# Layer norms, filters, feed and inverse transforms placed beside other stages, the spectral layer run by output parity, and pools that wait per tile

## The chip, the cores and the metric

The kernel runs on one core of a Trainium2 chip. Times are microseconds (us) of device time for one execution; the kernel before has a median of 3496.31 us over three runs. A profile is one execution taken by the hardware profiler. The engines are called PE (matmul; PEld is its weight load), DVE (vector), ACT (scalar, with the exponential), POOL and SP (which here only issues DMAs).

## The reference, cut to what matters

Two batches of 4096 tokens with 128 channels, all in float32:

```python
# layer 0: group norm, then 4 heads of 32 channels with 2-D rotary positions
xi  = group_norm(x)                               # (b, c, 4096)
q, k, v = split(w_qkv @ xi + b_qkv)               # q, k rotated and scaled
w   = softmax((q.T @ k).astype(float16))
x   = xi + w_proj @ (w @ v) + b_proj
# layer 1
t = x.transpose()                                 # (b, 4096, 128)
n = layer_norm(t)
t = t + softmax(n @ n.T) @ n                      # one head of 128, no weights
u = layer_norm(t)
t = t + sum_i weight[i] * pad(stu(u[:, :4096 // 2**i], i))   # weight: hard one-hot over 4
# stu: 16 filters phi_k convolved causally with u (and with u times (-1)^t),
#      mixed by two sets of 16 matrices, plus three taps M_u on u, u[t-1], u[t-2]
out = t.transpose()
```

The weights are a straight-through one-hot, so that the four branches become one with mixed matrices and a mask.

## The kernel before

The tokens of a batch are kept as `tok[b]`, 32 blocks of 128 tokens (partition = token). One program runs these stages one after another, on a matmul engine that executes in program order.

**Layer 0** (L146-346). Four units (batch, pair of heads). Each unit has 2 heads x 4 chunks of 1024 queries; for each of 32 key blocks two score matmuls (L315), one exp over 128x1024 (L323) and two weighted sums into `acc` (L282). Preparing the next unit (`rotate`, `values`) is a generator that is advanced by one step in every third key block (L335): `beside`. The last unit has none beside it. `rotate` loads a table `tab` (512 KB) through SP's queue (L181). `project` brings a finished chunk back to tokens (L261-265), eight matmuls `po`.

**Layer 1, attention** (L576-768). After layer 0 come the filter transforms (`ph`, L604-614: eight records of PE, copies on DVE, one store to DRAM as `tables`), the branch weights and coefficients, then `normalise` for both batches (L712): statistics by block, `pow` on POOL (L84), 32 normed blocks (L627), 32 transposes `yT` (L719) with copies on ACT. `self_attend` (L723) takes eight chunks of 512 queries; per pair of key blocks four f32 matmuls `y` (L742), two exps of 512 (L747) and, one pair later, four weighted sums `oacc` (L735). At each chunk's end come two of the sixteen `matrices` steps, which load `raw` through ACT's queue (L702) and sum it on DVE into `mx`. Then the residual, 32 operations on DVE (L766).

**Layer 1, feed** (L770-831). Per batch: layer norm into `un`, transforms of 512 columns `pf` (L781) stored to DRAM as `rows`, transposes of `un` and `tok` (L800, L801), three taps `ar` (L819) and the sum into `out[b]`. In program order feed 0 comes between the two attentions and feed 1 between attention 1 and the spectral layer.

**Spectral layer** (L841-958). Per batch eight chunks `ch` of 4 frequencies in each quarter. A chunk loads `tt` from `tables` and `ut` from `rows`, then runs four steps (output parity `ro`, stream `s`). A step is `convolve` (for each of 4 w: four matmuls of 32 rows into two 2-bank tiles `cv`, copied into `x` by DVE and ACT, L889) and `mix` (16 f32 matmuls of 512 columns, L899, accumulating both s in `acc`), which runs one step late, four matmuls after each w. After the second s `acc` is copied to `oh[ro]` (L905). After a batch's last step `back` (L910) transposes `oh` (`vt`), copies to `v`, applies the inverse transform `bk` (L929), adds to `out[b]` and stores it. In the PSUM pool `cv` has three tiles of two banks and `acc` two of one. The `tt` and `ut` loads go through SP, 10 for each half chunk (the page counts 256 and 384).

The order on each engine is set at build time by the program order and a planner that places an instruction when its inputs are due; each engine then runs its list in order and waits on semaphores. SP's DMAs use eight semaphores in turn, so that a DMA waits for the one eight before it. Pools that reuse memory of a closed pool wait for that whole pool.

Of the kernel before, what the change touches and what calls it, by code (L numbers as in the profile page):

```python
# [12 lines left out]
F32 = mybir.dt.float32  # L13
# [6 lines left out]
P = 128  # L20
# [9 lines left out]
NK = 16  # L30
# [28 lines left out]
def conv_attn_hybrid(ctx: ExitStack, tc: tile.TileContext, io):  # L59
# [26 lines left out]
    def group_norm(b, tok, bank, p1):  # L86


        xi = p1.tile([P, L], F32, tag="xi", name=f"xi{b}")
        xn = p1.tile([P, L], F32, tag="xn", name=f"xn{b}")  # L90
# [55 lines left out]
    def layer0(tok):  # L146
        with ExitStack() as l0:
            psum = l0.enter_context(tc.tile_pool(name="l0_psum", bufs=2, space=bass.MemoryType.PSUM))
            p1 = l0.enter_context(tc.tile_pool(name="l0_1", bufs=1))
            p2 = l0.enter_context(tc.tile_pool(name="l0_2", bufs=2))  # L150

            def bank(name):
                return psum.tile([P, 512], F32, tag="ms", name=name)
# [14 lines left out]
            def prepare(b, pr, xn):  # L168
# [9 lines left out]
                def rotate(i, hi, lo):  # L178
                    cols = bass.ts(i, 512)
                    tab = p2.tile([P, 2, 512], F32, tag="tab", name=f"tab{u}_{i}")  # L180
                    nc.sync.dma_start(tab, io["rot"][pr][:, :, cols])  # L181
# [88 lines left out]
            norm = group_norm(0, tok, bank, p1)  # L270
# [22 lines left out]
            def chain(*parts):  # L293
                for p in parts:
                    yield from p

            last = None
            for n, (b, pr) in enumerate(units):
                if n + 1 < len(units):
                    nxt = units[n + 1]  # L300
                    if nxt[1] == 0:
                        norm = group_norm(nxt[0], tok, bank, p1)
                        xn = next(norm)
                        after = prepare(*nxt, xn)
                        beside = chain(beside, norm, after[3], to_tokens(nxt[0], tok, xn, bank))
                    else:
                        after = prepare(*nxt, xn)
                        beside = chain(beside, after[3])
                for g in range(2):
# [35 lines left out]
            for _ in done:  # L345
                pass


    def layer0_any(tok):

        with ExitStack() as l0:
            p1 = l0.enter_context(tc.tile_pool(name="l0_1", bufs=1))
            p2 = l0.enter_context(tc.tile_pool(name="l0_2", bufs=2))
            p3 = l0.enter_context(tc.tile_pool(name="l0_3", bufs=3))

            psum = l0.enter_context(tc.tile_pool(name="l0_psum", bufs=2, space=bass.MemoryType.PSUM))

            def pair_bank(name):
                return psum.tile([P, 2, 512], F32, tag="st", name=name, bufs=2)

            def acc_bank(name):
                return psum.tile([P, 512], F32, tag="acc", name=name, bufs=1)

            def bank(name):
                return psum.tile([P, 512], F32, tag="ms", name=name, bufs=3)
# [14 lines left out]
            def normed(b):  # L380
                steps = group_norm(b, tok, bank, p1)
                xn = next(steps)
                for _ in steps:
                    pass
                for _ in to_tokens(b, tok, xn, bank):
                    pass
                return xn
# [168 lines left out]
            for n, (b, pr) in enumerate(units):  # L556
# [9 lines left out]
                k, v = k2, v2  # L566


    tables = dram.tile([NF, 2, 2, 2 * TROW], F32, name="tables")
    rows = [dram.tile([2, DROWS, NF, C], F32, name=f"rows{b}") for b in range(B)]  # L570

# [4 lines left out]
    def layers(st, layer0):  # L576
        held = st.enter_context(ExitStack())
        keep = held.enter_context(tc.tile_pool(name="keep", bufs=1, side="right"))

        tok = [keep.tile([P, NI, C], F32, name=f"tok{b}") for b in range(B)]  # L580
        layer0(tok)

        psum_1 = st.enter_context(ExitStack())
        psum = psum_1.enter_context(tc.tile_pool(name="psum", bufs=2, space=bass.MemoryType.PSUM))

        def pair_bank(name):
            return psum.tile([P, 2, 512], F32, tag="st", name=name, bufs=2)

        def acc_bank(name):
            return psum.tile([P, 512], F32, tag="acc", name=name, bufs=1)  # L590

        def bank(name):
            return psum.tile([P, 512], F32, tag="ms", name=name, bufs=3)

        fw = keep.tile([P, 4, NF], F32, name="fw")
        nc.sync.dma_start(fw, io["fw"])
        with tc.tile_pool(name="tab", bufs=1) as pt_:
            phi = pt_.tile([P, 2, TROW], F32, name="phi")  # L600
            nc.sync.dma_start(phi, io["phi"])
            tb = pt_.tile([P, 2, 2, 2 * TROW], F32, name="tb")
            tbr = tb.rearrange("w s i (o c k) -> w s i c o k", c=2, k=NK)
            for s in range(2):  # L604
                for c in range(2):
# [3 lines left out]
                    nc.vector.tensor_copy(tbr[:, s, 0, c], ph)  # L609
                    if c == 0:  # L610
                        nc.vector.tensor_copy(tbr[:, s, 1, 1], ph)
                    else:
                        nc.vector.tensor_scalar(tbr[:, s, 1, 0], ph, -1.0, None, ALU.mult)
            nc.sync.dma_start(tables, tb)


        def layer_norm(pool, src, dst, u, eps=1e-5):

            st = pool.tile([P, NT, 6], F32, tag="lst", name=f"lst{u}")
            mv = pool.tile([P, NT, 2], F32, tag="lmv", name=f"lmv{u}")  # L620
            for t in range(NT):
                nc.vector.bn_stats(st[:, t, :], src[:, t, :])
                nc.vector.bn_aggr(mv[:, t, :], st[:, t, :])
            rs = pool.tile([P, NT], F32, tag="lrs", name=f"lrs{u}")
            rstd_of(rs, mv[:, :, 1], 1.0, eps, NT)
            for t in range(NT):
                nc.vector.tensor_scalar(  # L627
                    dst[:, t, :], src[:, t, :], mv[:, t, 0:1], rs[:, t : t + 1], ALU.subtract, ALU.mult
                )

        ffw = st.enter_context(tc.tile_pool(name="ffw", bufs=1))
        mx = ffw.tile([P, NK, 2, C], F32, name="mx")
        gw = ffw.tile([P, 2, P], F32, name="gw")

        out = [ffw.tile([P, L], F32, name=f"out{b}") for b in range(B)]

        with ExitStack() as l1:
            p1 = l1.enter_context(tc.tile_pool(name="l1_1", bufs=1))

            def branch_weights(once):  # L640

                lg = p1.tile([P, 2, NBR], F32, name="lg")
                nc.gpsimd.dma_start(lg[:, 0, :], io["log_weights"].partition_broadcast(P))
                nc.gpsimd.dma_start(lg[:, 1, :], io["gumbel"].partition_broadcast(P))
                z = p1.tile([P, NBR], F32, name="z")
                nc.vector.tensor_tensor(z, lg[:, 0, :], lg[:, 1, :], ALU.add)
                zm = p1.tile([P, 1], F32, name="zm")
                nc.vector.tensor_reduce(zm, z, AX.X, ALU.max, negate=True)  # L650
                zs = p1.tile([P, 1], F32, name="zs")
                soft = p1.tile([P, NBR], F32, name="soft")
                nc.scalar.activation(soft, z, AF.Exp, bias=zm, accum_out=zs)
                nc.vector.reciprocal(zs, zs)
                nc.vector.tensor_scalar(soft, soft, zs, None, ALU.mult)
                sm = p1.tile([P, 1], F32, name="sm")
                nc.vector.reduce_max(sm, soft, axis=AX.X)
                top = p1.tile([P, NBR], F32, name="top")
                nc.vector.tensor_scalar(top, soft, sm, None, ALU.is_equal)
                free = p1.tile([P, NBR], F32, name="free")  # L660
                nc.vector.memset(free, 1.0)
                for i in range(1, NBR):
                    nc.vector.scalar_tensor_tensor(
                        free[:, i : i + 1], top[:, i - 1 : i], 0.0, free[:, i - 1 : i], ALU.is_equal, ALU.mult
                    )
                nc.vector.tensor_tensor(top, top, free, ALU.mult)
                wbr = p1.tile([P, NBR], F32, name="wbr")
                nc.vector.tensor_tensor(wbr, top, soft, ALU.subtract)
                nc.vector.tensor_tensor(wbr, wbr, soft, ALU.add)
                ends = once.tile([P, NBR, P], F32, name="ends")  # L670
                nc.gpsimd.dma_start(ends, io["ends"].partition_broadcast(P))
                mask = p1.tile([P, P], F32, name="mask")
                weighted_sum(mask, ends, top)
                return wbr, mask

            def weighted_sum(dst, src, w):

                nc.vector.tensor_scalar(dst, src[:, 0], w[:, 0:1], None, ALU.mult)
                for i in range(1, NBR):
                    nc.vector.scalar_tensor_tensor(dst, src[:, i], w[:, i : i + 1], dst, ALU.mult, ALU.add)  # L680

            mu = p1.tile([P, NU, C], F32, name="mu")
# [406 lines left out]
```

## Time and profile before

| | us |
|---|---|
| median of three runs | 3496.31 (3494.68 to 3497.91) |
| the profiled execution | 3495.54 |
| its span | 3493.7 |
| PE busy in it | 3345.4 |
| ACT busy | 1668.9 |
| DVE busy | 924.1 |
| POOL busy | 36.3 |

The granted PE clock is 0.983 of full speed on average. Stages in the span, read from the timeline:

| stretch, us | stage |
|---|---|
| 0 to 50 | loads, group norm, first preparation |
| 50 to 1114 | layer 0, four units |
| 1114 to 1188 | last projection, filters, coefficients, both norms, first y |
| 1188 to 1616 | attention 0 |
| 1616 to 2111.5 | attention 1, with feed 0 at its start |
| 2111.5 to 2227 | residual 1, feed 1, first convolve |
| 2227 to 2829.5 | spectral, batch 0 |
| 2829.5 to 2860 | inverse transform of batch 0 |
| 2860 to 3455 | spectral, batch 1 |
| 3455 to 3493.7 | inverse transform of batch 1, stores |

A busy time is the time in which the engine had an instruction in flight; for PE the ends are modelled, so a busy PE is not a PE at its peak. An idle gap costs time only on the engine that the rest waits for. The groups of waits name the instruction that waited, and the instruction or DMA that ended the wait.

### The profile page before, as it was taken

The numbers are of one execution on the slowest core, as the hardware profiler recorded it, in microseconds if no ns is written. First come the engines' busy times: TensorE is split into PE (matmuls) and PEld (weight loads), VectorE is DVE, ScalarE is ACT, GpSimd is POOL, SyncE is SP. The second block draws the span as 40 slices with busy tenths as digits, with TensorE's granted clock in tenths as the row PEclk, the third lists the DMA queues.
The fourth block names the chain that finished last, engine by engine and source line by source line (L and its number), as shares of the span: only waits on it lengthen the run. The fifth ranks groups of instructions, "written<-read, shape, count | busy, mean of one in ns | idle before, by whom it ended". The sixth has DMA issues, their size and how long they took to land.

```text
span 3493.7 us, 31758 instructions
## 1 busy us (share of the span) xinstructions
PE 3345.4 (96%) x12040; PEld 1542.3 (44%) x12040; DVE 924.1 (26%) x2010; ACT 1668.9 (48%) x2407; POOL 36.3 (1%) x36
## 2 busy tenths in 40 slices
PE   6999999999998799999999996899999999999998
PEld 3555555555554344444444442333333353333334
DVE  6621721611112620003100004222222232222222
ACT  2799799899997344444344442122222212222221
POOL 0000000000000100000000000000000000000000
PEclk9999999999999899999999998899999999999999
DMA  5300300300001110001000001423322222233300
GB/s 150 97 19 1 91 7 1 85 1 1 1 1 30 55 55 0 0 0 30 20 0 0 0 0 50 67 37 50 47 34 34 34 58 34 34 43 50 41 0 26
DMA packets 113796, 112.03 MB, mean 32 GB/s; under 512 B 17809, under 2 KB 77601, under 8 KB 113506
## 3 DMA queue, kind: packets, MB, share of 16 engines
q1 hardware_dynamic: 93056, 95.60, 14.6%
q10 hardware_dynamic: 19698, 11.81, 1.1%
q0 software_dynamic: 880, 2.50, 0.3%
q8 instruction: 97, 1.59, 0.2%
q14 instruction: 65, 0.53, 0.1%
HBM read 78.19 MB, written 14.88 MB: 27 GB/s over the span
## 4 chain that ended last, share of the span: by engine, by line
PE 83%; ACT 9%; DVE 4%; DMA 2%; issue 1%; POOL 1%; SPq 0%; ACTq 0%; POOLq 0%; DVEq 0%
PE m L899 27%; PE y L742 12%; PE oacc L735 12%; ACT e L323 9%; PE s L315 9%; PE cv L885 8%; PE acc L282 8%; PE po L261 1%; PE ar L819 1%; PE bk L929 1%; PE pv L206 1%; PE pb L183 1%; PE pa L190 1%; PE pf L781 1%; DVE tok L766 0%
## 5 line engine op out<-in xcount | busy, mean ns | idle before, releaser
L323 ACT ACTIVATE e<-s 128x1024 f16<-128x1024 f32 x1024 | 976.1, 1033 | 128.6 <-PE s L315 125.7
L899 PE MATMUL m<-x,mx 128*128 128x512 f32 x2048 | 947.8, 606 | 0.0
L889 ACT COPY x<-cv 128x1024 f32<-128x1024 f32 x256 | 259.1, 1012 | 944.7 <-PE cv L885 930.7
L899 PEld LDWEIGHTS m<-x,mx 128*128 128x128 f32 x2048 | 369.0, 190 | 561.3 <-issue 549.2
L315 PE MATMUL s<-qs,ks 128*128 128x512 f16 x2048 | 607.8, 379 | 6.1 <-ACT e L323 2.6
L282 PE MATMUL acc<-e,v 128*97 128x512 f16 x2048 | 604.5, 379 | 1.4 <-ACT e L323 1.0
L747 ACT ACTIVATE ey<-y,nshift 128x512 f32<-128x512 f32 x512 | 347.3, 683 | 525.8 <-PE y L742 523.7
L889 DVE COPY x<-cv 128x1024 f32<-128x1024 f32 x256 | 313.3, 1224 | 849.0 <-PE cv L885 849.0
L742 PE MATMUL y<-yT 128*128 128x512 f32 x1024 | 483.3, 594 | 0.0
L735 PE MATMUL oacc<-ey,y 128*128 128x512 f32 x1024 | 480.3, 593 | 0.0
L282 PEld LDWEIGHTS <-v 128*97 128x97 bf16 x2048 | 253.0, 124 | 215.1 <-issue 5.1
L885 PE MATMUL cv<-tt,ut 32*128 32x512 f32 x2048 | 310.6, 649 | 16.1 <-DMA ut<-rows 14.8
L735 PEld LDWEIGHTS oacc<-ey,y 128*128 128x128 f32 x1024 | 194.4, 190 | 242.0 <-issue 234.6
L742 PEld LDWEIGHTS y<-yT 128*128 128x128 f32 x1024 | 193.2, 191 | 232.9 <-issue 232.9
L315 PEld LDWEIGHTS <-ks 128*128 128x128 f16 x2048 | 199.8, 98 | 215.8 <-issue 108.8
L885 PEld LDWEIGHTS cv<-tt,ut 32*128 32x128 f32 x2048 | 86.5, 185 | 217.8 <-issue 205.7
L263 DVE RECIPROCAL rec<-po 128x1 f32<-128x1 f32 x256 | 42.7, 167 | 504.1 <-PE po L261 502.6
L756 DVE COPY oT<-oacc 128x512 f32<-128x512 f32 x16 | 11.0, 689 | 614.7 <-PE oacc L735 614.7
L261 PEld LDWEIGHTS po<-wp,accs 97*128 97x128 f32 x512 | 92.0, 192 | 37.9 <-DVE accs L290 9.2
L261 PE MATMUL po<-wp,accs 97*128 97x129 f32 x512 | 99.2, 282 | 4.4 <-DVE t L185 2.5
L747 ACT ACTIVATION_READ_ACCUMULATOR ey<-y,nshift 128x1 f32 x512 | 100.3, 196 | 0.0
L265 DVE SCALAR_TENSOR_TENSOR tok<-po,rec,tok 128x128 f32<-128x128 f32 x256 | 87.3, 348 | 6.8
(138 smaller groups left out, 1091.2 us busy)
## 6 DMA issues: line engine op xcount, KB each, us to landing
tt<-tables SPq DMA_DIRECT2D x256, 128.0 KB, 4.3
tab<-in_rot SPq DMA_DIRECT2D x32, 512.0 KB, 4.1
ut<-rows SPq DMA_DIRECT2D x384, 32.0 KB, 4.6
qs<-term SPq DMA_DIRECT2D x128, 64.0 KB, 2.0
ks<-term SPq DMA_DIRECT2D x128, 64.0 KB, 2.0
rows<-uh SPq DMA_DIRECT2D x64, 128.0 KB, 1.9
raw<-in_mpp ACTq DMA_DIRECT2D x16, 256.0 KB, 2.9
raw<-in_mpm ACTq DMA_DIRECT2D x16, 256.0 KB, 3.3
```

The lines of the kernel that those rows point to most:

```text
L261: nc.tensor.matmul(po, accs[:, t // 4, bass.ts(t % 4, P)], wp[:, h, :], start=True, stop=True)
L263: nc.vector.reciprocal(rec, po[:, C:])
L265: nc.vector.scalar_tensor_tensor(dst, po[:, :C], rec, dst, ALU.mult, ALU.add)
L282: nc.tensor.matmul(acc[: NV * CH + 1, q, :], v[:, t, g, :], e[:, q, :], start=(t == 0), stop=(t == NT - 1))
L315: nc.tensor.matmul(ps[:, q, :], ks[:, g, bass.ts(t, P)], qs[:, g, bass.ts(2 * c + q, 512)], start=True, stop=True,)
L323: nc.scalar.activation(e, ps, AF.Exp, scale=SCORE_SCALE)
L735: nc.tensor.matmul(acc, y[:, t, :], e[:, h, :], start=(t == 0), stop=(t == NT - 1))
L742: nc.tensor.matmul(ps[:, h, :], yT[:, bass.ts(t, P)], yT[:, bass.ts(i, 512)], start=True, stop=True)
L747: nc.scalar.activation(e[:, h, :], ps[:, h, :], AF.Exp, bias=nshift, accum_out=den[:, t, i : i + 1])
L885: nc.tensor.matmul(pu[:, h, :], ut[grp, w, q, :], tt[grp, w, s, :], start=True, stop=True)
L889: (nc.scalar.copy if g2 else nc.vector.tensor_copy)(x[:, :, at : at + 64].rearrange("d k (h c) -> d k h c", h=2), pu.rearrange("d h (c k) ...
L899: nc.tensor.matmul(acc, mx[:, k, s, :], x[:, k, :], start=(s == 0 and k == 0), stop=(s == 1 and k == NK - 1))
```

## The change

The sequence of stages stays, but much of what stood between them becomes generators that the attention and spectral loops advance by one step.

- All pools wait for the reuse of memory per tile. Layer 0 and attention share one PSUM pool (`st` 2 x 2 banks, `acc` 2 banks, `ms` 2 banks), and group norm's `xi`, `xn` share a pool with batch 0's `y` and `yT`.
- `normalise(0)` is advanced by layer 0's last unit, with DVE copying `yT`.
- Attention takes 1024 queries a chunk, one exp of 1024 columns per key block, and calls `next(beside)` in each of its 4 x 32 steps: `normalise(1)`, the filters and the matrices beside attention 0; the residual of batch 0 and feed 0 beside attention 1.
- The feed is cut in steps of four blocks. Its result is stored to DRAM (`base`) and loaded back (`had`) by `back`.
- The spectral layer runs by (batch, parity, chunk, s). `tt` and `ut` are loaded in every step, so 512 + 512 loads. `acc` and the new `bk` have one bank each. Feed 1 is advanced beside (0, 0), and `back` of each (batch, parity) beside the next one; the last has nothing beside it. At the end of each (batch, parity) the late mix and what is left beside are drained.
- The `tab` loads move from SP's queue to POOL's, the `raw` loads from ACT's to SP's.

```diff
+    def pool(stack, name, bufs=1, **kw):
+        return stack.enter_context(tc.tile_pool(name=name, bufs=bufs, reuse_waits="tile", **kw))
...
                     tab = p2.tile([P, 2, 512], F32, tag="tab", name=f"tab{u}_{i}")
-                    nc.sync.dma_start(tab, io["rot"][pr][:, :, cols])
+                    nc.gpsimd.dma_start(tab, io["rot"][pr][:, :, cols])
...
+                else:
+                    beside = beside_last()
                 for g in range(2):
...
+        def normalise(b, p, ytag, yttag):
...
+            def steps():
+                stats = layer_stats(p, tok[b], f"a{b}")
+                mv = next(stats)
+                yield from stats
+                for i in range(NQ):
+                    for t in range(4 * i, 4 * i + 4):
+                        normed(y[:, t, :], tok[b][:, t, :], mv, t)
+                    yield
+                    pt = bank(f"yT{b}_{i}")
+                    for t in range(4):
+                        nc.tensor.transpose(pt[:, bass.ts(t, P)], y[:, 4 * i + t, :], ident)
+                    nc.vector.tensor_copy(yT[:, bass.ts(i, 512)], pt)
+                    yield
...
+            late = None
+            for c in range(L // 1024):
+                acc = psum.tile([P, 2, 512], F32, tag="acc", name=f"oacc{b}_{c}", bufs=1)
+                for t in range(NT):
+                    ps = psum.tile([P, 2, 512], F32, tag="st", name=f"y{b}_{c}_{t}")
...
+                    nc.scalar.activation(e, ps, AF.Exp, bias=nshift, accum_out=den[:, t, c : c + 1])
+                    if late is not None:
+                        weigh(*late)
+                        if t == 0:
+                            close(c - 1, acc0)
+                    late = (acc, t, e)
+                    next(beside, None)
+                acc0 = acc
...
+        def feed(b, p, bank):
+            stats = layer_stats(p, tok[b], f"f{b}")
...
+            def taps(i, uT):
...
+                nc.scalar.copy(oc, pt)
+                yield
+                pa = bank(f"ar{b}_{i}").rearrange("p (t c) -> p t c", c=C)
+                for n in range(NU):
+                    nc.tensor.matmul(pa, mu[:, n, :], uT[:, 2 - n : 6 - n, :], start=(n == 0), stop=(n == NU - 1))
+                    if n + 1 < NU:
+                        yield
+                nc.vector.tensor_tensor(oc, pa, oc, ALU.add)
+                nc.sync.dma_start(base[b][:, 4 * i : 4 * i + 4, :], oc)
+                yield
...
+                o, den = attend(0, p1, *ys[0], chain(steps, filters(p), matrices(p)))
...
+                o, den = attend(1, p1, *ys[1], chain(residual(0, p1, o, den), feed(0, p, bank)))
+            for _ in residual(1, p1, o, den):
+                pass
...
+            tt = pi.tile([P, WC, 2 * BP * NK], F32, tag="tt", name=f"tt{u}", bufs=3)
+            ut = pi.tile([P, WC, C], F32, tag="ut", name=f"ut{u}", bufs=4)
...
+        def back(b, ro, oh, outs, p):
...
+            for p4 in range(BP // 4):
+                nc.sync.dma_start(had, baser[:, ro, 4 * p4 : 4 * p4 + 4, :])
...
+                for c in range(2):
+                    pt = one_bank(f"vt{u}_{c}").rearrange("p (q c) -> p q c", c=C)
+                    for q in range(4):
+                        nc.tensor.transpose(pt[:, q, :], ohr[:, c, BP - 1 - 4 * p4 - q, :], ident)
+                    (nc.scalar.copy if c else nc.vector.tensor_copy)(v[:, c, :, :], pt)
+                    yield
+                pt = one_bank(f"bk{u}").rearrange("p (q j) -> p q j", j=P)
+                for q in range(4):
+                    for c in range(2):
+                        nc.tensor.matmul(pt[:, q, :], v[:, c, q, :], gw[:, c, :], start=(c == 0), stop=(c == 1))
+                nc.vector.tensor_tensor(outr[:, ro, 4 * p4 : 4 * p4 + 4, :], pt, had, ALU.add)
+                yield
...
+        beside = feed(1, late_pool, one_bank)
+        for b in range(B):
+            for ro in range(2):
+                oh = po.tile([P, L], F32, tag="oh", name=f"oh{b}_{ro}")
+                for ch in range(NCH):
+                    acc = pc.tile([P, 512], F32, tag="acc", name=f"m{b}_{ro}_{ch}")
+                    for s in range(2):
+                        tt, ut = chunk(b, ro, ch, s)
...
+                        for _ in convolve(u, tt, ut, x):
+                            next(late, None)
+                            next(beside, None)
+                        late = mix(ch, s, x, acc, oh)
+                for _ in chain(late, beside):
+                    pass
...
+                beside = back(b, ro, oh, outs, late_pool)
+        for _ in beside:
+            pass
```

## Prediction

> **What bounds the kernel now.** I read the page's slices first, then busy time by windows cut where the stages meet, then the waits of the tensor engine, then the timeline at two seams.
>
> ```profile
> PE   6999999999998799999999996899999999999998
> PEclk9999999999999899999999998899999999999999
> ```
>
> The tensor engine is the bound nearly everywhere, and it dips in four places: at the start, near slice 13, near slice 25 and at the end. The granted clock dips with it.
>
> ```profile
> 850.00:1114.00 264.00, 263.19 (x1245) 141.34 (x1243) 44.98 (x156) 260.57 (x276) 0.00 (x0) 1.00 0.00 1
> 1114.00:1188.00 74.00, 37.28 (x124) 20.57 (x125) 52.46 (x264) 15.37 (x37) 16.32 (x9) 0.72 0.18 58
> 1188.00:1616.00 428.00, 428.00 (x1019) 190.09 (x1017) 45.55 (x110) 178.61 (x494) 0.00 (x0) 1.00 0.06 19
> 1616.00:2111.50 495.50, 488.53 (x1209) 220.37 (x1207) 52.51 (x167) 202.18 (x538) 5.53 (x2) 1.00 0.03 9
> 2111.50:2227.00 115.50, 67.74 (x196) 29.90 (x196) 45.24 (x148) 21.60 (x30) 5.43 (x1) 0.76 0.40 75
> 2860.00:3455.15 595.15, 595.15 (x2005) 222.67 (x2004) 158.19 (x133) 129.51 (x131) 0.00 (x0) 1.00 0.23 34
> ```
>
> Columns: window, length, busy time of PE, PEld, DVE, ACT, POOL, granted clock, DMA share, GB/s. Steady attention and steady spectral work leave PE no gap. The two seams, 1114-1188 (layer norms and filters between layer 0 and attention 0) and 2111.5-2227 (residual and feed of batch 1 before the spectral layer), hold only 37 and 68 us of PE in 190. The last unit of layer 0 is held by ACT too: 260.57 of 264.
>
> ```profile
> PE pf L781 <- DVE un L627: 28.1, 2, 22.5
> PE yT L719 <- issue: 24.2, 1, 24.2
> PE gn_mean L103 <- DVE gmv L99: 19.5, 1, 19.5
> PE cv L885 <- DMA ut<-rows: 14.8, 3, 7.4
> ```
>
> The largest waits of PE. Three of the four lie in those seams; gn_mean is the kernel's head, which the change hardly touches.
>
> ```profile
> 3418.00 1.14 PE L885 MATMUL cv<-tt,ut 32*128 32x512 f32 x8
> 3419.07 3.70 PE L899 MATMUL m<-x,mx 128*128 128x512 f32 x8
> 3422.70 1.14 PE L885 MATMUL cv<-tt,ut 32*128 32x512 f32 x8
> 3422.81 0.69 DVE L905 COPY oh<-m 128x512 f32<-128x512 f32 x1 [2.41 <-PE m L899]
> 3423.77 3.70 PE L899 MATMUL m<-x,mx 128*128 128x512 f32 x8
> ```
>
> Start, length, engine, line: one w of the spectral layer starts every 4.70 us, so a step of four w is 18.8 us, and 64 steps are 1203.2.
>
> **The sum, by stretches.** PE's work is priced by start spacing: an f32 matmul record of 512 columns 0.4285 us (two records a matmul), a 128-column transpose 0.11. The number of matmuls does not change; what changes is what stands between them.
>
> *Layer 0's end to attention 0's end* took 1616.0-1114.0 = 502.0. In the changed program's instruction order the statistics, normed blocks and 32 transposes of batch 0 stand between layer 0's last scores, attention's first y follow the last acc, and batch 1's norm, the filters and the matrices come one step at a time between y and oacc. What is left there: 1024 records x 0.4285 = 438.8, o transposes 32 x 0.11 = 3.5, yT of batch 1 3.5, filters 8 x 0.42 = 3.3 and the last projection 2.6: 451.7, so -50.3. The cover is 128 steps of 3.43 us on PE, of which one 1024-wide exp takes ACT about 1.23 (1.03, the L323 row, plus a 0.20 read); DVE's 8.2 us of statistics and 8.3 of normed blocks are small beside them. Without the cover the 45 us of gap come back. The transposes moved into layer 0 cost 3.5 at face value: ACT and PE are both full there; between 0 (the 3.4 us in which ACT idles take them) and 8 (each of 8 groups also delays an exp by 0.5). A wait for POOL's pow (5.43 us) stands ahead of transposes two steps later, about level with it; I add 2 for such waits, range 0 to 6. Net -45.
>
> *Attention 1* took 495.5. Work: 438.8 + 3.5 + feed 0 (pf 32 and ar 48 records x 0.4285, 64 transposes, pl 0.4: 41.7) = 484.0, plus 2 for the same waits: -9.5. Feed's 75 steps fit in 128.
>
> *From 2111.5 to the end* took 1382.2. Afterwards:
> - Start. The first x copy on DVE stands behind the o copies (3 us) and 32 residual operations (0.266 each, 8.5), and the next ones between 8.2 us of statistics and a normed block that waits for the 5.43 us pow. Adding two steps' copies (8 x 1.22 = 9.8) and 1.0 for that block: DVE needs 36 us, in which PE has 14.5 to do. Loss 21.5; between 12 (residual alone in the way) and 30 (the statistics of the next blocks ahead as well).
> - 64 steps 1203.2, feed of batch 1 41.7 within the first 16 of them.
> - Three inverse transforms beside the next steps: 32 transposes and 64 records of bk (14.6 us for 128 in the tail): 3.5 + 7.3 = 10.8 each, 32.4.
> - The three ends of a (batch, parity), where the last mix is drained before the next cv. The first has the rest of feed 1 (11 of 75 steps do not fit in 64) in series with its one PSUM bank: 21.5 us to the next mix, of which 15 is work, so 6.5. The others 4 each (x copies at 1.22 a w, no mix beside). 14.5 in all, between 0 and 25.
> - Tail: only one parity is left, but over one bank in series: per block vt 0.65, copy 0.75, vt 0.65, copy 0.7, eight bk 2.0, add 1.2 = 5.95, four times and a first copy: 24.5. From the last add to the end 11.0 as now (3482.7 to 3493.7). 35.5, against 38.5 now.
>
> Sum 1348.8, -33.4.
>
> *The single accumulator.* Its two banks become one, so the first mix of a step waits for L905's copy. The rows above: copy ends at 3423.50, next mix starts at 3423.77, 0.27 to spare. Cost between 0 and 32 x 1.0 us (if DVE or ACT is in a 1.2 us copy or add when it is due); I take 3, because the copy is queued ahead of the next x copy. Behind it stand all sixteen mixes, so this stall would go straight to the end.
>
> *Loads.*
>
> ```profile
> tt<-tables SPq DMA_DIRECT2D x256, 128.0 KB, 4.3
> tab<-in_rot SPq DMA_DIRECT2D x32, 512.0 KB, 4.1
> ut<-rows SPq DMA_DIRECT2D x384, 32.0 KB, 4.6
> ```
>
> (Tile, queue, count, KB, us to landing.) tt doubles to 512 loads, ut becomes 512: 16 a step. A burst of ten takes SP 5.65 us in the timeline, so 16 take 9.0 of the step's 18.8, two steps ahead of use; the share, 0.23 to 0.29, would come near 0.5. The rows and base stores of feed 1 stand among them in SP's order and wait for ACT and DVE, but the loads beside them are for two steps later: nothing, unless a load is over 37 us late. The 32 raw loads go from ACT's queue to SP's during attention 0, a pair at a time (2.9 and 3.3 us to landing there now); mx is needed only 500 us later, so nothing. The feed's result makes a trip to DRAM (16 stores and 16 loads of 256 KB, on SP too), each a whole (batch, parity) ahead of its use: nothing. The 32 tab loads leave SP for POOL, behind the xi loads there; nothing else of weight waits on POOL. xi landed in 8.1 us from POOL and 8.7 from SP, so I take 0, between -3 and +8 (eight exposed loads, 1 us each, in the head).
>
> The Trainium skill has a rule against that move ("SBUF — State Buffer", section "SBUF: two separate sides"): loads issued by GpSimd have descriptors written in software, and a two-port VectorE operation locks it out, 620 ns becoming 3100. No row here shows it. By that rule, an estimate, the eight loads of the head would be 2.5 us late each, and the sum up to 20 higher.
>
> The windows at 0.72 and 0.76 are the clock's row. "TensorE: Matmul & The Clock Gate" (Part 1) has the array at half rate until one window of about 3.4 us was busy. By it, an estimate, each of the five idle places left would cost 1.7 more, 8.5 on the sum; I price no such term.
>
> In all -45 - 9.5 - 33.4 + 3 = -85 against the profiled execution's 3495.54 (span 3493.7), which is 0.8 under the median of 3496.31: **3411** on the median.
>
> **Rivals.**
> - *More hidden than I charge:* start 12, ends 0, layer 0's transposes and the waits free: 9.5 + 14.5 + 3.5 + 4 + 3 = 34 less, 3377. For: DVE's low share. Against: the order of DVE at the start.
> - *The spectral seams and the single bank take back a third:* 32 x 1.0 instead of 3, start 30, ends 25: +29 + 8.5 + 10.5 = 3459 at worst, about 3445. For: 0.27 us of slack is thin with other work on DVE. Against: that slack was there in every step.
> - *Slower: the spectral loads become the bound.* At most eight DMAs are under way on SP's semaphores, so a step needs 16/8 landings. It decides above 18.8 + 85/64 = 20.1 us a step, 1.26 a load, a landing of 10.1 us instead of 4.5. At 11.2 us a step is 22.4: 64 x 3.6 = +230, 3641. For: in the crowded head tab landed in 4.1 to 14.4 us, median 7.5. Against: the spectral stage moves only 41 GB/s, the head 169.
> - *It does not do what it says:* a norm or feed still stands ahead of the next stage on an engine. Both big seams kept, the smaller ends give about 3490.
>
> **How the numbers follow.** Forecast 0.62, more hidden 0.12, a third back 0.14, slower 0.09, not as said 0.03. No change means within 0.2%, 7 us: only the last case and the edge of the slower one, 0.02. Faster 0.90, slower 0.08. The range leaves out the slower case and the last, and reaches into the two near ones: 3375 to 3450.
>
> **What would show it.** PE gaps at the two big seams gone, with about 20 us at the spectral start behind DVE; y and oacc back to back at 3.43 us; steps of 18.8 with mix waiting under 0.3 for oh; cv waiting for no DMA; tail near 35. Wrong if steps are longer than 19.5, if PE waits for tt, or if layer 0 ends over 8 us later.

## The result and the profile after

The changed kernel takes 3985.61 us (3981.06 to 3993.36, four runs) against 3497.11 for the kernel before in the same session: 1.14 times as long, 95% interval 1.138 to 1.142. The forecast of 3411 and its range were wrong, and in sign.

The page's slices of the kernel after, PE's busy tenths and its granted clock:

```profile
PE   6999999999998999999999999999999999999997
PEclk9999999999999999999989998987798777877777
```

The dips of PE at the two big seams are gone. In their place the clock falls in the last third, where PE looks busy. The stretches of the kernel after, in the columns of the windows before, cut where its own stages meet:

```profile
1115.00:1582.70 467.70, 456.70 (x1103) 204.11 (x1102) 84.47 (x284) 154.68 (x258) 5.53 (x2) 0.99 0.14 32
1582.70:2067.90 485.20, 485.20 (x1205) 219.28 (x1203) 49.15 (x172) 168.86 (x282) 5.53 (x2) 1.00 0.05 16
2130.00:2430.00 300.00, 300.00 (x1001) 119.06 (x1000) 84.74 (x103) 67.87 (x78) 0.00 (x0) 1.00 0.42 73
3055.00:3260.00 205.00, 186.16 (x388) 70.86 (x388) 32.00 (x27) 24.88 (x25) 0.00 (x0) 0.75 0.27 39
3950.20:3991.50 41.30, 19.87 (x97) 16.75 (x96) 6.83 (x8) 2.93 (x5) 0.00 (x0) 0.70 0.18 65
```

Both attentions are done at 2067.9 instead of 2111.0: 43 us were won up to there. The first parity of the spectral layer (third row) gives PE 3.3 records a microsecond at full clock; a later stretch (fourth row) 1.9 at 0.75. From the last `oacc` to the end the kernel before took 1383 us, the changed one 1924. All of the loss is there.

The length of a step is easiest to read off the copies of `oh`, one for every two steps (a pair). One in the kernel before, whose next is the row at 3422.81 that the prediction shows, then two neighbours in the kernel after:

```profile
3385.19 0.58 ACT L905 COPY oh<-m 128x512 f32<-128x512 f32 x1 [2.56 <-PE m L899]
```

```profile
3085.03 0.69 DVE L937 COPY oh<-m 128x512 f32<-128x512 f32 x1 [4.92 <-PE m L931]
3152.56 0.59 ACT L937 COPY oh<-m 128x512 f32<-128x512 f32 x1 [20.64 <-PE m L931]
```

Times between such copies in us, within a (batch, parity):

| stretch | before | after |
|---|---|---|
| (0,0), feed 1 beside | 37.6 | 42.8 |
| (0,1), first four pairs after its first | 37.6 | 43.6, 46.7, 39.3, 68.2 |
| later | 37.6 | 56.7 to 68.2, mostly near 68 |

A late step is 34.1 us, not 18.8. One of them in the timeline of the kernel after (start, length, engine, line, records, idle before), with weight loads and SP's rows left out:

```profile
3112.36 6.28 PE L931 MATMUL m<-x,mx 128*128 128x512 f32 x14
3118.57 1.98 PE L920 MATMUL cv<-tt,ut 32*128 32x512 f32 x8
3119.76 1.23 DVE L922 COPY x<-cv 128x1024 f32<-128x1024 f32 x1 [6.01 <-PE cv L920]
3121.04 1.13 PE L920 MATMUL cv<-tt,ut 32*128 32x512 f32 x4 [0.49 <-DVE x L922]
3122.21 1.23 DVE L922 COPY x<-cv 128x1024 f32<-128x1024 f32 x1 [1.23 <-PE cv L920]
3123.49 7.38 PE L920 MATMUL cv<-tt,ut 32*128 32x512 f32 x16 [1.33 <-DVE x L922]
3125.83 1.01 ACT L922 COPY x<-cv 128x1024 f32<-128x1024 f32 x1 [27.55 <-PE cv L920]
3127.49 1.01 ACT L922 COPY x<-cv 128x1024 f32<-128x1024 f32 x1 [0.65 <-PE cv L920]
3129.20 1.01 ACT L922 COPY x<-cv 128x1024 f32<-128x1024 f32 x1 [0.69 <-PE cv L920]
3129.26 1.23 DVE L922 COPY x<-cv 128x1024 f32<-128x1024 f32 x1 [5.82 <-PE cv L920]
3130.90 1.01 ACT L922 COPY x<-cv 128x1024 f32<-128x1024 f32 x1 [0.69 <-PE cv L920]
3131.97 2.08 PE L931 MATMUL m<-x,mx 128*128 128x512 f32 x2 [1.10 <-ACT x L922]
```

Before, four m followed every w, and the copies lay under them. Here nearly all of a step's cv come in one block: PE runs up to three PSUM tiles ahead, then at the pace of the copies, DVE's first and ACT's four after, and the m that should cover them have been used up or wait for the block's last copy. From 3118.57 to 3131.97 PE does work worth about 4 us: 28 records of cv, of which eight took 1.14 us before. The two records of m behind the block take 1.0 us each instead of 0.43: the clock has been halved.

The list of PE as built, one line a step (a, b: a half of cv of the first and second group of rows; M: one m), shows the same before anything runs:

```
(0,0) chunk 3, s 1   aabbMMMMaabbMMMMaabbMMMMaabbMMMM
(0,1) chunk 2, s 0   aaMbMMMaabMMMbbMaabbMMMMaabbMMMM
(0,1) chunk 5, s 0   aMMMMMMMMaMMMMMMMbaabaabbbbaabbM
(1,1) chunk 5, s 0   aMMMMMMMMaMMMMMMMbaabaabbbbaabbM
```

The trace runs cv and m in the same order. One half of cv slips behind four m from (0,1) chunk 1 on, the order comes apart at chunk 2, and from chunk 4 on it has the shape of the last two lines in all but a few steps at the start of each parity. The largest waits of PE in the kernel after, over the whole run (instruction, what ended the wait, total us, count, longest us):

```profile
PE cv L920 <- DVE x L922: 65.1, 73, 2.3
PE m L931 <- ACT x L922: 38.6, 35, 1.1
PE gn_mean L110 <- DVE gmv L106: 20.0, 1, 20.0
PE ph L663 <- DVE tb L667: 7.3, 1, 7.3
```

The first two rows are mostly such blocks; they add up to 104 us, far less than the loss, because a PE that is paced by copies or runs at half clock counts as busy. Two rows of SP's queue in the same kernel from 2700 to 3800 us, in the same columns:

```profile
SPq L902 <- PE cv L920: 645.4, 28, 25.7
SPq L902 <- DMA tt<-tables: 46.4, 98, 1.2
```

PE never waits for a spectral load. SP issues its 16 in some 9 us and then waits up to 25.7 us for PE to give a tile back. tt landed in 4.6 us at the median (4.3 before). So the loads are not late on the chip; the suspicion falls on the planner, which decided the order at build time as if they were.

### The profile page after: what moved, and what is told of

It reads as the page before. It is cut to its first block, busy times and chain, and to the rows that moved or that the text cites. A ratio compares the mean times of both kernels' runs of the same rounds, so it can differ in the third digit from the quotient of the medians.

```text
span 3991.5 us, 32076 instructions
## 1 busy us (share of the span) xinstructions
PE 3807.7 (95%) x12032; PEld 1729.9 (43%) x12032; DVE 927.9 (23%) x2040; ACT 1592.5 (40%) x1879; POOL 59.1 (1%) x68
## 4 chain that ended last, share of the span: by engine, by line
PE 75%; issue 12%; DVE 6%; ACT 4%; DMA 2%; POOL 1%; SPq 0%; DVEq 0%; POOLq 0%; ACTq 0%
PE m L931 26%; PE cv L920 15%; PE y L764 10%; PE oacc L745 10%; PE s L317 5%; PE acc L286 4%; ACT e L325 3%; DVE x L922 2%; DMA raw<-in_mpm 1%; PE ar L809 1%; PE bk L961 1%; ACT x L922 1%; PE pf L826 1%; PE po L265 1%; DVE pm L596 1%
## 5 line engine op out<-in xcount | busy, mean ns | idle before, releaser
L931 PE MATMUL m<-x,mx 128*128 128x512 f32 x2048 | 1053.8, 665 | 39.8 <-ACT x L922 38.6
L920 PE MATMUL cv<-tt,ut 32*128 32x512 f32 x2048 | 660.4, 776 | 66.3 <-DVE x L922 65.1
L931 PEld LDWEIGHTS m<-x,mx 128*128 128x128 f32 x2048 | 411.6, 211 | 686.4 <-issue 584.4
L768 ACT ACTIVATE ey<-y,nshift 128x1024 f32<-128x1024 f32 x256 | 285.3, 1114 | 596.9 <-PE y L764 596.9
L920 PEld LDWEIGHTS cv<-tt,ut 32*128 32x128 f32 x2048 | 221.9, 218 | 430.1 <-issue 233.4
L937 ACT COPY oh<-m 128x512 f32<-128x512 f32 x16 | 9.4, 586 | 233.5 <-PE m L931 233.5
```

The lines of the kernel that those rows point to most:

```text
L768: nc.scalar.activation(e, ps, AF.Exp, bias=nshift, accum_out=den[:, t, c : c + 1])
L920: nc.tensor.matmul(pu[:, h, :], ut[grp, w, :], tt[grp, w, :], start=True, stop=True)
L931: nc.tensor.matmul(acc, mx[:, k, s, :], x[:, k, :], start=(s == 0 and k == 0), stop=(s == 1 and k == NK - 1))
```

## The experiments

Theory A: the order of cv and m in PE's list is the cost. Theory B: the doubled loads are, on the chip. Theory C: a PE that is never idle is granted less clock.

**e1_pinned.** Each cv and m gets an edge to the one before it in the written order, which fixes the order of issue and adds no semaphore.

```diff
-                        nc.tensor.matmul(pu[:, h, :], ut[grp, w, :], tt[grp, w, :], start=True, stop=True)
+                        pin(nc.tensor.matmul(pu[:, h, :], ut[grp, w, :], tt[grp, w, :], start=True, stop=True))
```

> Theory A (order): what costs the time is the order of cv and m on PE from (0,1) chunk 2 on, which differs from the order written. Here the same 16 loads a step stay on SP and PE's cv and m keep the order written (aabb, four m, four times a step). A expects steps of 18.8 us and 3400 to 3430. Theory B (loads): the doubled loads on SP are late on the chip; it expects steps near 34 us still, cv waiting for tt or ut, and about 3985. Theory C (clock): a PE that is busy without a break is granted less clock; it expects the granted clock near 0.76 in the spectral layer, steps of 18.8/0.76 = 24.7 us, and about 3411 + 46 x 5.9 = 3680.

Measured 3452.82 (ratio to before 0.9884, interval 0.9867 to 0.990), granted clock 0.988, pairs of steps at 37.6. With the same loads on the same queue, 533 us of the loss are gone. It misses A's upper end by 23 us: where two parities meet the distance is 64.9 and 63.2, against 53.2 to 53.4 in the next two runs, probably because the instructions of `back`, which were not pinned, still bunch there (vt waits 16.7 us in all, 8.5 in e2_ut_pool); no run pins them. One window of it, in the columns of the windows before:

```profile
2860.00:3065.00 205.00, 205.00 (x696) 76.38 (x694) 55.61 (x47) 46.00 (x47) 0.00 (x0) 1.00 0.54 75
```

**e2_ut_pool.**

```diff
-                    nc.sync.dma_start(ut[part, :, :], rows[b][ci, row : row + BP, w0 : w0 + WC, :])
+                    nc.gpsimd.dma_start(ut[part, :, :], rows[b][ci, row : row + BP, w0 : w0 + WC, :])
```

> The 512 ut loads go through POOL's queue, tt stays on SP (8 loads a step there, as many bytes in all); nothing is pinned, and the built order of PE is then the one written. A expects 3400 to 3430, and equal to e1_pinned within 10 us. B expects a gain too, by the share of SP's loads taken away, but steps above 18.8. C expects about 3680.

Measured 3427.4 (0.98, 0.9784 to 0.9817).

**e3_ut_merged.**

```diff
-                    nc.sync.dma_start(ut[part, :, :], rows[b][ci, row : row + BP, w0 : w0 + WC, :])
+                nc.sync.dma_start(ut[32 * g : 32 * g + 32, :, :], rows[b][:, row : row + BP, w0 : w0 + WC, :])
```

> The two ut loads of a group are made one of twice the size: 12 loads a step on SP, the same bytes; the built order of PE is the one written. A expects 3400 to 3430. B expects 12/16 of the added delay, about 3840. C expects about 3680.

Measured 3428.74 (0.9798, 0.9782 to 0.9815). Both times are where A puts them, but e2_ut_pool is 25 us from e1_pinned, where A expected at most 10; B would have 3840 here. In e2_ut_pool steps of 18.8 run at full clock with the DMA engines busier than in the changed kernel (0.56 against 0.27 in its late stretch) and PE never idle, which also ends C. One window of it, in the columns of the windows before:

```profile
2860.00:3065.00 205.00, 205.00 (x691) 76.91 (x690) 53.50 (x45) 43.67 (x44) 41.95 (x88) 1.00 0.56 71
```

**e4_order**, **e5_order_exact**, **e9_one_half** put the bad order back on e2_ut_pool's light queue, each closer to the list of the changed kernel. These three and e6_fourteen are single executions. The step as written out in the last, condensed and with comments added:

```diff
+                half(0, 0, 0)          # w, group, half
+                yield 8                # so many m
+                half(0, 0, 1)
+                yield 7
+                half(0, 1, 0); half(1, 0, 0); half(1, 0, 1); half(1, 1, 0); half(2, 0, 0); half(2, 0, 1)
+                half(2, 1, 0); half(0, 1, 1); half(1, 1, 1); half(2, 1, 1)
+                half(3, 0, 0); half(3, 0, 1); half(3, 1, 0); half(3, 1, 1)
+                yield 1
```

> The loads of e2_ut_pool, but cv and m of every step from (0,1) chunk 2 on are put in the order that the changed kernel's list has there (one cv half, 8 m, one half, 7 m, then the other 14 halves by group). A expects steps of about 34 us in these 44 steps and 3950 to 4000, like the changed kernel. B and C expect what they expect of e2_ut_pool.

3714.52: too little. Its last m of a step belonged to the step before.

> e4_order came to 3714.5, half way only. In it the m at the end of a step was the last of the step before; in the changed kernel's list it is the first m of the step itself, which waits for the step's last copy. Here that is put right, the loads as in e2_ut_pool. Theory A, with the order as the whole cause: steps near 34 us, PE at half clock for 500 us or more, 3900 to 4000. Rival: the order accounts for 290 us only and the rest comes from the 16 loads on SP; then this stays at 3700 to 3750.

3836.01: the m is right and the time is still 150 us short, which left the rival standing.

> In the changed kernel's list of a late step the first half of cv (w 2, second group) stands ahead of the second halves of (w 0) and (w 1), and waits for DVE's copy of (w 2, first group); e5_order_exact had it behind them. Here it is put ahead; the loads as in e2_ut_pool (8 a step on SP). Theory A, the order as the whole cause: ACT's first copy of a step comes about 4 us later, the step goes from 30 to 34 us, half clock for 17 us of each step, and 3960 to 4000, the changed kernel's time. Rival, the loads on SP make the missing 150 us: 3836 as in e5_order_exact.

4035.0, with pairs of 68.2 as in the changed kernel (50 us over it; 37 of them lie in (0,1), where the bad order sets in at once at chunk 2, while the changed kernel reaches it at chunk 4). The stretch that was shown of the changed kernel, in e9_one_half:

```profile
3055.00:3260.00 205.00, 187.47 (x388) 71.21 (x387) 30.08 (x25) 25.46 (x26) 22.89 (x48) 0.75 0.30 39
```

With half as many loads on SP the order alone makes all of the loss. That one half of cv is worth 200 us: it waits for DVE, and the second halves for w 0 and w 1 of ACT's group stand behind it in PE's list. Much of the 200 can be clock: the granted clock is 0.939 over 3834.2 us in e5_order_exact and 0.911 over 4033.2 us in e9_one_half, 468 and 718 us at half clock, which is up to 125 us of the difference.

**e6_fourteen.** ut merged for two of the four groups.

> 14 loads a step on SP: the two ut loads are merged for two of the four groups. The built order is as written until (1,0) chunk 1 and then turns into that of the changed kernel, so 29 of 64 steps have it. Theory A: those 29 at about 32 to 34 us, 3427 + 29 x 12.7 = 3800 (3740 to 3830), the steps before them at 18.8. Theory B, a cost of each load on the chip: all steps alike, between e3_ut_merged (12 loads) and e1_pinned (16), 3430 to 3450.

3725.64, clock 0.949: pairs of 37.6 up to (0,1) chunk 5, from (1,0) chunk 4 on 60 to 61.5 but for one of 49.3. That is the bad order of A, at 30.7 a step instead of 32 to 34, so the total came out below A's band. B's equal steps are not there. The order holds with 8 and 12 loads a step on SP, and with the 10 of the kernel before (256 + 384 loads for 64 steps), and tips with 14 and 16. If the planner charges every load alike and the order tips when the charges exceed a step, which no run shows, an estimate of the charge is above 18.8/14 = 1.34 us and at most 18.8/12 = 1.57, while ten loads took 5.65 us on the chip, 0.57 each.

The remaining three follow up what was mis-sized, each on top of the last.

**e7_filters**, on e3_ut_merged (comment added):

```diff
-                weighted_sum(pm, raw, coef[:, k, :])
+                with tc.issue_after(filtered[0].ins):      # the last tb copy
+                    weighted_sum(pm, raw, coef[:, k, :])
```

> e3_ut_merged, and the sums of the matrices on DVE are queued behind the last copy of the filters. In e2_ut_pool and e3_ut_merged PE stood about 10 us at ph, whose copies stood on DVE behind a sum that waited for its raw load, and ran two windows at half clock after it. Theory: attention 0 ends 10 to 14 us earlier, 3415 to 3420. Rival (the gap is merely moved to the matrices): no change, 3425 to 3430.

3412.61 (0.975, 0.9734 to 0.9767). The cause, in e2_ut_pool's timeline: DVE's copies of the filters stand behind a sum that waits for its raw load, so PE waits at ph for 7.45 us and y resumes at half clock.

```profile
1231.04 0.35 DVE L594 TENSOR_SCALAR pm<-raw,coef 128x256 f32<-128x256 f32 x1 [3.53 <-DMA raw<-in_mpm]
1231.43 1.52 DVE L596 SCALAR_TENSOR_TENSOR pm<-raw,coef,pm 128x256 f32<-128x256 f32 x3
1232.87 0.67 DVE L665 COPY tb<-ph 128x496 f32<-128x496 f32 x1
1233.46 0.66 DVE L667 COPY tb<-ph 128x496 f32<-128x496 f32 x1
...
1234.27 1.99 PE L663 MATMUL ph<-phi,fw 128*128 128x496 f32 x2 [7.45 <-DVE tb L667]
1236.05 2.75 PE L764 MATMUL y<-yT 128*128 128x512 f32 x4
```

**e8_both**: the last inverse transform takes its banks from the cv tiles (comment added).

```diff
+            bank = wide_bank if (b, ro) == (B - 1, 1) else one_bank      # a bank of a cv tile, bufs=3
```

> e7_filters, and the last inverse transform takes its banks from the three cv tiles, which are free by then, in place of one bank. If the single bank is what holds the tail, the 42 us from the last m to the end become 28 to 34, and the time 8 to 14 less than e7_filters: 3402 to 3412. If the half clock or the stores hold it, within 3 us of e7_filters.

3397.37 (0.9717, 0.9701 to 0.9733), 15 less; the last m to the end fell from 42.6 to 27.3. The single bank held the tail, and part of the 15 is clock: in that stretch the granted clock rose from 0.62 to 0.83.

**e10_start**:

```diff
-                    (nc.scalar.copy if g2 else nc.vector.tensor_copy)(
+                    (nc.scalar.copy if g2 or u.startswith("0_0_0") else nc.vector.tensor_copy)(
```

> e8_both, and the copies of x in the first two spectral steps all go to ACT, which is idle there, in place of every second one to DVE. If the first m is late because those copies stand behind the residual and the statistics on DVE (the start term of the prediction, 20.8 us from the last oacc to the first m), the first m comes after about 12 us and the time is 6 to 12 less than e8_both, 3385 to 3392. If it is the o copies or the loads that hold it, within 3 us of e8_both.

3376.4 (0.9654, 0.9638 to 0.967), 21 less, about twice what was expected. The first m came after 12.2 us instead of 20.8, and PE kept its clock there. The two profiles are 18.2 us apart: 12.2 are won by the first copy of `oh`, and 6.3 where (0,0) meets (0,1). There PE's instructions stand in the same order in both, but e8_both spends 13.7 us at half clock and e10_start none; the edit does not reach that place, so this part is luck as far as the runs tell. The window at the start of the spectral layer in e8_both, in the columns of the windows before:

```profile
2051.00:2072.00 21.00, 13.60 (x50) 4.68 (x50) 21.00 (x89) 4.05 (x4) 0.00 (x0) 0.70 0.12 20
```

The same window in e10_start: PE busy 18.7 us instead of 13.6, ACT 11.2 instead of 4.1, clock 1.00 instead of 0.70.

```profile
2051.00:2072.00 21.00, 18.72 (x78) 6.99 (x76) 18.57 (x99) 11.19 (x12) 2.31 (x1) 1.00 0.38 51
```

It is the fastest version found, 3.5% under the kernel before.

## Why the prediction was wrong

The step that failed is "64 steps 1203.2", together with "nothing" for the doubled loads. It priced a step by the timeline of the kernel before, and so took that order of cv and m as given for all 64. The prediction cites the changed program's instruction order for the seam into attention 0 and not for the spectral steps, where it holds as written through nearly all of the first parity and is lost in the 46 steps from (0,1) chunk 1 on. What the runs showed in its place: late steps of 34.1 us, and 18.8 again once the order is pinned with all 16 loads in place. The price of the loads was asked of the chip's queue (9.0 us of 18.8, which the runs bear out: PE never waited for one), and not of the planner that lays out the list. That the planner reckons a higher price is inferred from which load counts tip the order; that the order is the cost is shown. The rival for the slower side, loads as the bound on the chip, named the right part of the change and the wrong place: landing stayed at 4.6 us, far from its 10.1, and the stall is PE behind DVE and ACT.

e2_ut_pool holds what the rest of the sum was worth, with the order as assumed: 3427.4 against the forecast 3411, -66 in the span against -85. The 19 us between them are the balance of terms that were off both ways:

- *To attention 0's end*, forecast -45: -33 (467.1 against 502.0, and layer 0 1.4 longer). The term of 2 for waits was mis-sized: the filters' copies behind the raw loads cost most of the 12 more. e7_filters has 451.2 from the last acc to the end of attention 0; the work was put at 451.7.
- *Attention 1*, forecast 484 + 2: 485.3.
- *Spectral start*, forecast a loss of 21.5: in e2_ut_pool 63.6 us to the first oh copy, where one cv block of 4.3 and two steps of 21.4 make 47: 16.6 lost. e10_start shows the named cause, DVE's queue.
- *Steps*: 37.6 a pair, and 42.8 with feed 1, as forecast where the order is the written one.
- *Single accumulator*, forecast 3: nothing; away from feed 1 and from the first and last pairs of a parity they are 37.6 to the tenth in all kernels with the written order.
- *Ends of the parities*, forecast 14.5: about 23.5 (1317.4 us from the last oacc to the last m, less 1203.2, 41.7, 32.4 and 16.6).
- *Tail*, forecast 35.5: 42.6. The mechanism was right (e8_both), but PE ran it at a granted clock of 0.62, for which the sum had no term.
- *tab on POOL*, forecast 0: landing 4.2 us on the page after, 4.1 before; the first scores begin at 47.6 to 51.7 us in the runs and at 48.2 before. The delay that the Trainium skill's "SBUF — State Buffer" (section "SBUF: two separate sides") led to fear did not show, nor for the 512 ut loads of e2_ut_pool: they landed in 5.2 us, against 4.5 from SP in the changed kernel, and the pairs have the lengths that they have in e3_ut_merged, within 1.2 us. DVE's `x` copies beside them read PSUM, so this says nothing of other copies.

The clock was given no term. The Trainium skill's page "TensorE: Matmul & The Clock Gate" (Part 1) was right to ask for one: the granted clock in the trace is 1 or 0.5 and nothing else, and every low stretch up to the tail is a multiple of 3.41 us long, the length of that page's window. Within the span they sum to 120 us before, 84 in e2_ut_pool, 21 in e10_start, and 667 in the changed kernel, 17.1 of most late steps of 34.1. The late step's 15.3 us of loss is therefore at most 8.5 of clock; the rest is the block itself. e4_order shows a block without the clock, in its own milder order: a pair with no low stretch took 46.6, 4.5 a step over 18.8. The late pairs also keep time with the low stretches: 68.2 is twenty times 3.41, and the 61.4 of e6_fourteen eighteen times; no run tests why.

## What to carry to other kernels

Where a planner lays out the engines' lists, read the built order of the steady loop to its end, at its last step too, before pricing it by a timeline: a change that adds loads can change the order of matmuls though no load is ever late. If the planner's price for an issue is above the chip's, fewer and larger loads (e3_ut_merged), a second queue (e2_ut_pool), or edges that pin the written order (e1_pinned) keep the list. Work moved beside another stage inherits that stage's queue: look for the DMA wait that it now stands behind.

## What the runs showed of the hardware that was not expected

A PE that is 91% busy in the profile can run half its time at half clock: in 3055 to 3260 us of the changed kernel it was busy 186 of 205 us at 0.75. In the late step shown no wait of PE is longer than 1.33 us, yet in 13.4 us it had work worth 4, and the clock was halved 4.7 us into that block. It came back 8.4 us after the next m began; in the steps with 17.1 us at half clock that took 7 to 10 us. A gap removed can thus be worth more than its length: in e10_start 8.6 us less before the first m made 12.2 by the first copy of `oh`.
